# Layer 1 written out as four pipelines, layer 2's constants loaded inside it, and reciprocal square roots by Newton steps

## The chip, the cores and the metric

One Trainium2 chip; the program runs on 1 core. The core's engines each work through a queue of their own: TensorE (PE: matmuls and transposes; its weight loads are listed as PEld), VectorE (DVE), ScalarE (ACT), GpSimd (POOL) and SyncE (SP, which here only issues transfers). A result passes between engines through SBUF or through TensorE's accumulator banks (PSUM), and a semaphore tells the next engine that it is there. The metric is the device time of one execution in microseconds.

## The reference

The program is a network of four layers on x of shape (2, 64, 64, 128): two images, 64 x 64 positions, 128 channels. Cut to what the change touches:

```python
# layer 1: x = x + L1(groupnorm(x)), 32 groups of 4 channels
def L1(x):                                   # (b, 64, 64, 128)
    xn = layer_norm(x, norm_a, norm_b)       # over the 128 channels
    left  = (xn @ Wl + bl) * sigmoid(xn @ Wlg + blg)
    right = (xn @ Wr + br) * sigmoid(xn @ Wrg + brg)
    out_gate = sigmoid(xn @ Wog + bog)
    out = einsum('bkjd,bkid->bijd', left, right) / 64
    out = layer_norm(out, on_a, on_b) * out_gate
    return out @ Wo + bo

# layer 2, attention: t = t + L2(layer_norm(t)), t = x as (2, 4096, 128), 4 heads of 32
def L2(x):
    q, k, v = silu(x @ Wq + bq), silu(x @ Wk + bk), silu(x @ Wv + bv)
    u = x @ Wu + bu
    pos = einsum('nm,bmd->bnd', pos_w[4095 + m - n], v)      # Toeplitz, not causal
    s = where(causal, (q @ k.T / sqrt(32)) ** 2, 0)
    a = concat(silu(s) @ v, pos)
    a = layer_norm(a) * ln_gamma + ln_beta
    return relu(u * a @ Wf + bf) + x
```

Layer 0 is a groupnorm and a softmax attention with relative positions over the 4096 positions, layer 2 has an expert layer behind the attention, and layer 3 is an attention and an expert layer. Each of them starts with a norm, so each needs 1/sqrt(variance + eps). Everything is in float32.

## The kernel before

x stays in SBUF throughout, as 64 tiles of 128 positions x 128 channels. The layers run one after the other; the order of the work on each engine is mostly the order in which the program issues it, as a scheduler places it, and inside layers 0 and 2 it is written out by generators that yield between pieces (a stage's filling work is cut in pieces, and so many pieces are issued between two steps of the main loop).

**1/sqrt** is `rstd_parts`, lines 95 to 112. VectorE adds eps (line 101, tile rs_v), ScalarE takes the square root (line 105, rs_s), VectorE takes the reciprocal (line 108, rs_r) and sharpens it by one Newton step of three operations (lines 110 to 112). ScalarE holds one set of function tables at a time, and going from the sigmoid, silu or exponential to the square root and back shows as an ACT_TABLE_LOAD. `ln_stats` (lines 149 to 159) calls it for n tiles at once, after a pair of bn_stats and bn_aggr (lines 155, 156) for each; `group_scale` calls it for a groupnorm on 128x1.

**Layer 1** (lines 1044 to 1186) has five stages.
- Normalisation, lines 1067 to 1104. For each of the two images: `group_stats` transposes 32 tiles and takes their statistics, and two matmuls spread mean and scale over all partitions (line 1071, l1pb), which VectorE copies to gb (line 1079). Then four groups of 8 tiles: VectorE subtracts the mean (line 1083, l1y), POOL multiplies by the scale (line 1089), VectorE takes the row statistics and normalises (line 162), TensorE transposes (line 1098, l1pt), ScalarE writes xnT with norm_a and norm_b (line 1102).
- Projections, lines 1110 to 1126, 64 steps j. The weights of both matmuls are the columns j, j+64, ... of xnT, a strided read. VectorE adds the biases (lines 1117, 1118), ScalarE takes two sigmoids (1119, 1120), VectorE multiplies left and right by their gates into lr, with stride 64 (line 1121).
- Triangle product, lines 1129 to 1147: 256 matmuls of 64 x 64 x 64 for each of both halves, evicted by ScalarE (line 1142).
- Output norm, lines 1149 to 1169, 8 groups of 8: row statistics, 8 normalisations, multiplication by on_a and addition of on_b on VectorE (lines 1155, 1158), the gate product on POOL (line 1161), transposes (1166) and their copies on ScalarE (1167).
- Output projection, lines 1171 to 1186: 16 groups of 4 matmuls (l1o); POOL adds bo to x (line 1183), VectorE adds the result (line 1186).

**Layer 2's attention** starts with its constants (lines 1237 to 1278): a reversed position table of 2 MB is loaded (rev), TensorE flips it with an anti-diagonal matrix (line 1263, l2flip), and VectorE writes it less its last value to toe (line 1264). `l2_folded` (lines 1189 to 1228) loads six small tensors and folds ln_gamma, ln_beta, Wu and Wf into wuy and buy (l2fT, l2ub, l2fy). Then come the weights and biases of q, k and v. The main loop goes over 16 blocks of 512 queries; scores are evicted by VectorE (line 1551) or ScalarE (line 1541) into l2es, POOL squares some of them in place (line 1554), ScalarE applies silu (line 1565), and TensorE multiplies by v (line 1579). Each block ends with a norm that calls `rstd_parts` on 128x4.

Of the kernel before, what the change touches and what calls it, by code (L numbers as in the profile page):

```python
# [8 lines left out]
F32 = mybir.dt.float32  # L9
AF = mybir.ActivationFunctionType  # L10
ALU = mybir.AluOpType
# [3 lines left out]
P = 128  # L15
# [23 lines left out]
class Net:  # L39
# [57 lines left out]
    def rstd_parts(self, out, var, eps, n, apart=False):  # L97
# [6 lines left out]
        s = self.small.tile([P, n], F32, tag=f"rs_s{n}", name="rs_s", bufs=4 if n < 8 else 2)  # L104
        nc.scalar.activation(s, v, AF.Sqrt)
        yield
        r = self.small.tile([P, n], F32, tag=f"rs_r{n}", name="rs_r", bufs=4 if n < 8 else 2)
        nc.vector.reciprocal(r, s)
        q = self.small.tile([P, n], F32, tag=f"rs_q{n}", name="rs_q", bufs=4 if n < 8 else 2)
        nc.vector.scalar_tensor_tensor(q, r, -0.5, r, ALU.mult, ALU.mult)  # L110
        nc.vector.tensor_tensor(q, q, v, ALU.mult)
        nc.vector.scalar_tensor_tensor(out, q, 1.5, r, ALU.add, ALU.mult)
# [48 lines left out]
    def normalize(self, out, src, mv, r, i):  # L161
        self.nc.vector.tensor_scalar(
            out, src, mv[:, i, 0:1], r[:, i : i + 1], ALU.subtract, ALU.mult
        )
# [879 lines left out]
    def layer1(self):  # L1044
        nc, tc, ins = self.nc, self.tc, self.ins
        with ExitStack() as st:
            wp = st.enter_context(tc.tile_pool(name="l1w", bufs=1))
            ps = st.enter_context(tc.tile_pool(name="l1p", bufs=3, space=PSUM))
# [16 lines left out]
            xnT = big.tile([P, B * L], F32, tag="a", name="l1xnT")  # L1065
            with tc.tile_pool(name="l1y", bufs=2) as yp:
                for b in range(B):
                    gm, gr = self.group_stats(ps, b)
# [9 lines left out]
                    gb = yp.tile([P, 2, C], F32, tag="gb", name=f"l1gb{b}")  # L1078
                    nc.vector.tensor_copy(gb.rearrange("p i c -> p (i c)"), pb[:, : 2 * C])
                    for g in range(4):  # L1080
                        ch = b * NC + 8 * g
                        y = yp.tile([P, 8, C], F32, tag="y", name=f"l1y{b}_{g}")
                        nc.vector.tensor_tensor(
                            y,
                            self.x[:, ch : ch + 8, :],
                            gb[:, 0, :].unsqueeze(1).broadcast_to([P, 8, C]),
                            ALU.subtract,
                        )
                        nc.gpsimd.tensor_tensor(
                            y, y, gb[:, 1, :].unsqueeze(1).broadcast_to([P, 8, C]), ALU.mult  # L1090
                        )
                        mv, r = self.ln_stats(y, 8, 1e-5, f"l1_{b}_{g}")
                        for half in range(2):
                            pt = ps.tile([P, 512], F32, tag="misc", name=f"l1pt{b}_{g}_{half}")
                            for k in range(4):
                                i = 4 * half + k
                                self.normalize(y[:, i, :], y[:, i, :], mv, r, i)
                                nc.tensor.transpose(
                                    pt[:, k * P : (k + 1) * P], y[:, i, :], self.ident
                                )  # L1100
                            at = (ch + 4 * half) * P
                            nc.scalar.activation(
                                xnT[:, at : at + 512], pt, AF.Identity, bias=nb, scale=na
                            )


            lr = big.tile([P, 2, C, S], F32, tag="lr", name="lr")
            gate = big.tile([P, S, C], F32, tag="gate", name="gate")
            with tc.tile_pool(name="l1t", bufs=3) as tp:
                for j in range(S):  # L1110
                    rows = xnT[:, j::S]
                    p1 = ps.tile([P, 512], F32, tag="misc", name=f"l1p1_{j}")
                    nc.tensor.matmul(p1, lhsT=rows, rhs=wcat[:, :512], start=True, stop=True)
                    p2 = ps.tile([P, C], F32, tag="og", name=f"l1p2_{j}")
                    nc.tensor.matmul(p2, lhsT=rows, rhs=wcat[:, 512:], start=True, stop=True)
                    t = tp.tile([P, 5 * C], F32, tag="t", name=f"l1t{j}")
                    nc.vector.tensor_tensor(t[:, :512], p1, bcat[:, :512], ALU.add)  # L1117
                    nc.vector.tensor_tensor(t[:, 512:], p2, bcat[:, 512:], ALU.add)
                    nc.scalar.activation(t[:, 256:512], t[:, 256:512], AF.Sigmoid)
                    nc.scalar.activation(gate[:, j, :], t[:, 512:], AF.Sigmoid)  # L1120
                    nc.vector.tensor_tensor(
# [4 lines left out]
                    )  # L1126

            tri = big.tile([P, S, C], F32, tag="a", name="tri")
            for d8 in range(C // 8):
                pt = ps.tile([P, 8, S], F32, tag="misc", name=f"l1tri{d8}")  # L1130
                for k in range(8):
# [10 lines left out]
                nc.scalar.activation(  # L1142
                    tri[:, :, 8 * d8 : 8 * d8 + 8].rearrange("p j d -> p d j"),
                    pt,
                    AF.Copy,
                    scale=1.0 / S,
                )
            yT = big.tile([P, B * S, S], F32, tag="lr", name="l1yT")
            for g in range(S // 8):
                js = slice(8 * g, 8 * g + 8)  # L1150
                mv, r = self.ln_stats(tri[:, js, :], 8, 1e-5, f"l1o{g}")
                for i in range(8):
                    self.normalize(tri[:, 8 * g + i, :], tri[:, 8 * g + i, :], mv, r, i)
                tj = tri[:, js, :]
                nc.vector.tensor_tensor(
                    tj, tj, ona.unsqueeze(1).broadcast_to([P, 8, C]), ALU.mult
                )
                nc.vector.tensor_tensor(
                    tj, tj, onb.unsqueeze(1).broadcast_to([P, 8, C]), ALU.add
                )  # L1160
                nc.gpsimd.tensor_tensor(tj, tj, gate[:, js, :], ALU.mult)
# [1057 lines left out]
```

## Time and profile before

| | |
|---|---|
| time, median of 3 runs | 4488.38 us (4481.65 to 4494.05) |
| the profiled execution's own time | 4491.71 us |
| its span on the profile | 4489.8 us |
| mean granted TensorE clock | 0.938 |
| TensorE (PE) busy | 4093.3 us (91%) |
| VectorE (DVE) busy | 2932.6 us (65%) |
| ScalarE (ACT) busy | 2488.6 us (55%) |
| GpSimd (POOL) busy | 912.0 us (20%) |
| layer 0 | 0 to 1606.6 us |
| layer 1 | 1606.6 to 1903.6 us |
| layer 2's constants | 1903.6 to 1946.6 us |
| layer 2's attention, main loop | 1946.6 to 3106 us |
| the rest | 3106 to 4489.8 us |

In a line of the profile, L1117 is line 1117 of the kernel, and out<-in names the tile written and the tiles read, with partitions x elements. A group's line gives how many instructions there were, their busy time in us and the mean of one in ns, and then how long the engine was idle just before them and what ended that. A table by stage gives for each stretch its length and each engine's busy time, with the granted TensorE clock and the share of time in which the DMA engines were busy. A busy TensorE is not TensorE at its peak.

### The profile page before, as it was taken

Reading aid. Unit: us, or ns where it says so; the run is one execution under the profiler, and the core shown is the slowest. Engines: PE = TensorE matmul, PEld = TensorE weight load, DVE = VectorE, ACT = ScalarE, POOL = GpSimd, SP = SyncE. Lnnn points to the kernel's source line nnn. Section 1 sums busy time; section 2 is a strip of 40 time slices with the busy share of each in tenths; the row PEclk is TensorE's granted clock in tenths of the full one; section 3 lists DMA queues with packets and bytes.
Section 4 is the critical chain, followed back from the end, with each engine's and each line's share of the span. In section 5 each row is a group of like instructions: output and inputs, shape, how many; then the busy total and the mean of one; then the engine's idle time right before and its main releaser. Section 6 shows DMA issues by size and latency. Waiting matters only on the chain.

```text
span 4489.8 us, 66995 instructions
## 1 busy us (share of the span) xinstructions
PE 4093.3 (91%) x26440; PEld 1633.4 (36%) x26440; DVE 2932.6 (65%) x4641; ACT 2488.6 (55%) x3267; POOL 912.0 (20%) x667
## 2 busy tenths in 40 slices
PE   6999999999999948468999899998689999999979
PEld 3233333333333326322233223332364444444453
DVE  4888888998999979745566656656253333333358
ACT  3777777777777724235777688785123222322225
POOL 4110011020000030113455455552000000000015
PEclk7999999999999968678999999997889999999969
DMA  6453335454333300000000000002610000000001
GB/s 174 93 135 62 69 84 137 76 123 89 59 60 61 61 9 1 10 18 1 1 1 1 1 1 1 1 1 88 177 40 0 0 0 1 0 0 1 0 10 34
DMA packets 200764, 189.10 MB, mean 42 GB/s; under 512 B 83546, under 2 KB 137658, under 8 KB 200250
## 3 DMA queue, kind: packets, MB, share of 16 engines
q1 hardware_dynamic: 196986, 179.35, 18.1%
q10 hardware_dynamic: 3072, 4.34, 0.4%
q8 instruction: 210, 3.44, 0.3%
q0 software_dynamic: 384, 1.05, 0.1%
q14 instruction: 112, 0.92, 0.1%
HBM read 143.78 MB, written 45.09 MB: 42 GB/s over the span
## 4 chain that ended last, share of the span: by engine, by line
PE 47%; DVE 9%; ACT 4%; issue 1%; SPq 1%; DMA 1%; POOL 0%; DVEq 0%; ACTq 0%; POOLq 0%
PE oTl L1954 10%; PE scl L1937 10%; PE l2sc L1527 5%; PE l2pos L1428 5%; PE l2av L1579 5%; PE f3ex L2121 2%; ACT l2es L1565 2%; SPq L1682 1%; PE l2pu L1412 1%; DVE l2es L1551 1%; DVE l1t L1117 1%; ACT l2es L1541 1%; PE l2po L1486 1%; PE l3pq L1889 1%; PE prl L1976 1%
## 5 line engine op out<-in xcount | busy, mean ns | idle before, releaser
L813 DVE TENSOR_TENSOR l0acc<-l0acc,l0es 128x1024 f32<-128x1024 f32 x960 | 1230.6, 1282 | 133.1 <-ACT l0es L808 39.3
L808 ACT ACTIVATE l0es<-l0sc 128x1024 f32<-128x1024 f32 x1024 | 952.4, 1053 | 284.7 <-PE l0sc L800 267.8
L800 PE MATMUL l0sc<-l0mv,ka 64*64 64x512 f32 x8192 | 921.7, 596 | 21.1 <-DMA l0mv<-l0hd 16.3
L1962 DVE TENSOR_TENSOR accl<-accl,esl 128x1024 f32<-128x1024 f32 x240 | 294.0, 1225 | 520.1 <-ACT esl L1948 482.1
L1554 POOL TENSOR_TENSOR l2es<-l2es 128x1024 f32<-128x1024 f32 (+3 forms) x288 | 505.0, 1753 | 603.9 <-DVE l2es L1551 532.8
L1948 ACT ACTIVATE esl<-scl 128x1024 f32<-128x1024 f32 x240 | 245.5, 1023 | 547.0 <-PE scl L1937 547.0
L1565 ACT ACTIVATE l2es<-l2es 128x1024 f32<-128x1024 f32 (+3 forms) x576 | 533.3, 977 | 6.9 <-POOL l2es L1558 6.7
L800 PEld LDWEIGHTS l0sc<-l0mv,ka 64*64 64x64 f32 x8192 | 294.5, 132 | 640.9 <-ACT l0es L808 296.8
L1551 DVE TENSOR_SCALAR l2es<-l2sc 128x1024 f32<-128x1024 f32 (+3 forms) x272 | 306.4, 1126 | 297.2 <-PE l2sc L1527 294.5
L1937 PE MATMUL scl<-l3qT,l3kT 128*128 128x512 f32 x1024 | 482.4, 593 | 0.9 <-DVE l3v L1903 0.9
L831 PE MATMUL l0o<-l0es,l0v 128*32 128x512 f32 x4096 | 465.6, 595 | 0.0
L1954 PE MATMUL oTl<-esl,l3v 128*128 128x512 f32 x960 | 448.5, 592 | 0.0
L1541 ACT ACTIVATE l2es<-l2sc 128x1024 f32<-128x1024 f32 (+3 forms) x288 | 273.4, 949 | 261.3 <-PE l2sc L1527 258.2
L1527 PE MATMUL l2sc<-l2q,l2kT 32*128 32x512 f32 (+3 forms) x2304 | 340.5, 625 | 10.0 <-DVE l2es L1551 5.8
L1579 PE MATMUL l2av<-l2es,l2v 128*32 128x512 f32 (+3 forms) x2304 | 321.6, 579 | 8.8 <-ACT l2es L1565 8.7
L1428 PE MATMUL l2pos<-l2v,toe 128*32 128x512 f32 (+3 forms) x2304 | 299.5, 581 | 1.4 <-ACT l2v L1373 1.4
L745 POOL TENSOR_TENSOR l0os<-l0os,l0rr 128x512 f32<-128x512 f32 x32 | 63.2, 1975 | 1152.0 <-ACT l0rr L742 1091.3
L2133 POOL TENSOR_TENSOR f3part<-f3part 128x256 f32<-128x256 f32 x64 | 46.5, 726 | 1204.3 <-ACT f3part L2130 1204.3
L1937 PEld LDWEIGHTS scl<-l3qT,l3kT 128*128 128x128 f32 x1024 | 192.2, 190 | 231.1 <-issue 226.5
L1954 PEld LDWEIGHTS oTl<-esl,l3v 128*128 128x128 f32 x960 | 182.4, 190 | 229.6 <-issue 225.5
L831 PEld LDWEIGHTS l0o<-l0es,l0v 128*32 128x32 f32 x4096 | 121.4, 109 | 304.1 <-issue 299.5
L1527 PEld LDWEIGHTS l2sc<-l2q,l2kT 32*128 32x128 f32 x2304 | 100.9, 189 | 255.0 <-ACT l2es L1565 91.7
(468 smaller groups left out, 3915.6 us busy)
## 6 DMA issues: line engine op xcount, KB each, us to landing
l0mv<-l0hd SPq DMA_DIRECT2D x254, 128.0 KB
l0mv<-l0qd SPq DMA_DIRECT2D x124, 256.0 KB
f2w<-in_L_ffn_weight_dram SPq DMA_DIRECT2D x16, 1024.0 KB
f2w<-in_L_ffn_weight_dram SPq DMA_DIRECT2D x64, 256.0 KB
l0mv<-l0wd SPq DMA_DIRECT2D x126, 128.0 KB
l0sh<-l0eh SPq DMA_DIRECT2D x60, 144.0 KB
l0tw<-l0sw SPq DMA_DIRECT2D x64, 128.0 KB
l0wd<-l0rw SPq DMA_DIRECT2D x16, 512.0 KB
```

Of the source, the lines that this page charges most:

```text
L800: nc.tensor.matmul(sc[64 * c : 64 * c + 64, h, :], lhsT=ka[rows, k0 : k0 + 64], rhs=mv[rows, NX - 1 - yb, :], start=True, stop=True,)
L808: nc.scalar.activation(es[yb, s], sc, AF.Exp)
L813: nc.vector.tensor_tensor(cur.acc, cur.acc, es[yb, s], ALU.add)
L831: nc.tensor.matmul(cur.o[lo : lo + HD, :], lhsT=v[:, 2 * (xb * NX + yb) + s, HD * h : HD * (h + 1)], rhs=es[yb, s][:, h, :], start=(xb == ...
L1428: nc.tensor.matmul(pos[c : c + 32, j0:, :], lhsT=toe[:, d * P + c : d * P + c + 32], rhs=v[:, n0 + j0 - d : n0 + 4 - d, :], start=(d == n0 ...
L1527: nc.tensor.matmul(sc[:, h2, off:], lhsT=kT[hs, cols], rhs=q[hs, off:], start=True, stop=True,)
L1551: nc.vector.tensor_scalar(es[:, :, lo:], sc[:, :, lo:], root, None, ALU.mult)
L1554: nc.gpsimd.tensor_tensor(part, part, part, ALU.mult)
L1565: nc.scalar.activation(e[:, :, off:], e[:, :, off:], AF.Silu)
L1579: nc.tensor.matmul(avs[i][hs, off:], lhsT=vs[b][:, k, hs], rhs=es[h // 2][:, h % 2, off:], start=(k == 0), stop=last,)
L1937: nc.tensor.matmul(sc[:, i, :], lhsT=kT[:, k * P : (k + 1) * P], rhs=qs, start=True, stop=True,)
L1954: nc.tensor.matmul(oT, lhsT=v[:, k, :], rhs=es[:, i, :], start=(k == 0), stop=(k == NC - 1),)
```

## The change

`rstd_parts` takes no square root on ScalarE any more: a first guess comes from the bits of the variance, read as an integer (one VectorE operation), and three Newton steps of three VectorE operations follow. It yields after the first of them.

`layers12` replaces layer1 and layer2_attn. It opens the pool of layer 2's constants first, and hands layer 1 a generator, `l2_constants`, which layer 1 runs inside its normalisation: the loads at its start (after layer 1's own, on SP's queue), the flips in the last three rounds of its loop, `l2_folded` after that, with its loads on ScalarE's queue. The table of 2 MB lies in the buffer that later holds lr.

Layer 1 is written in the order of emission (manual_schedule):
- normalisation: all of `group_stats` in pieces; then a loop over rounds s, in which POOL subtracts and multiplies for group s (shift), ScalarE writes xnT for group s-3 (turned), 6 of 8 normalisations of group s-2 are ScalarE's and 2 VectorE's (rows), and the row statistics are those of group s-1. There is a y buffer for each of the 8 groups and PSUM has 5 buffers instead of 3. xnT is written as [partition, j, image, i], so that a step's weights are contiguous.
- projections: the gate's bias addition goes straight to gate, the product into lr is POOL's, and POOL adds bo to x every fourth step.
- triangle product: evicted by VectorE and ScalarE in turn.
- output norm: a loop over rounds, with the 8 normalisations on ScalarE and the multiplication by on_a on POOL; on_b stays on VectorE and the gate product on POOL.
- output projection: without the addition of bo.

```diff
@@ rstd_parts
-        s = self.small.tile([P, n], F32, tag=f"rs_s{n}", name="rs_s", bufs=4 if n < 8 else 2)
-        nc.scalar.activation(s, v, AF.Sqrt)
-        yield
         r = self.small.tile([P, n], F32, tag=f"rs_r{n}", name="rs_r", bufs=4 if n < 8 else 2)
-        nc.vector.reciprocal(r, s)
+        nc.vector.tensor_scalar(
+            r.bitcast(mybir.dt.int32),
+            v.bitcast(mybir.dt.int32),
+            -0.5,
+            float(0x5F3759DF),
+            ALU.mult,
+            ALU.add,
+        )
         q = self.small.tile([P, n], F32, tag=f"rs_q{n}", name="rs_q", bufs=4 if n < 8 else 2)
-        nc.vector.scalar_tensor_tensor(q, r, -0.5, r, ALU.mult, ALU.mult)
-        nc.vector.tensor_tensor(q, q, v, ALU.mult)
-        nc.vector.scalar_tensor_tensor(out, q, 1.5, r, ALU.add, ALU.mult)
+        for i in range(3):
+            nc.vector.scalar_tensor_tensor(q, r, -0.5, r, ALU.mult, ALU.mult)
+            nc.vector.tensor_tensor(q, q, v, ALU.mult)
+            nc.vector.scalar_tensor_tensor(out if i == 2 else r, q, 1.5, r, ALU.add, ALU.mult)
+            if i == 0:
+                yield
@@ new helpers
+    def shifts(self, mv, r, n):
+        m = self.small.tile([P, n], F32, tag=f"lm{n}", name="lm")
+        self.nc.vector.scalar_tensor_tensor(m, mv[:, :, 0], -1.0, r, ALU.mult, ALU.mult)
+        return m
+
+    def normalize_act(self, out, src, r, m, i):
+        self.nc.scalar.activation(
+            out, src, AF.Identity, bias=m[:, i : i + 1], scale=r[:, i : i + 1]
         )
@@ layer 1, normalisation
+                def shift(s):
+                    b, g = divmod(s, 4)
+                    ch = b * NC + 8 * g
+                    for i, op in enumerate((ALU.subtract, ALU.mult)):
                         nc.gpsimd.tensor_tensor(
+                            ys[:, s],
+                            ys[:, s] if i else self.x[:, ch : ch + 8, :],
+                            gbs[b][:, i, :].unsqueeze(1).broadcast_to([P, 8, C]),
+                            op,
+                        )
...
+                for s in range(B * 4 + 3):
+                    if s == 1:
+                        group_rows(1)
+                    if s < B * 4:
+                        shift(s)
+                    if 3 <= s:
+                        turned(s - 3)
+                    if 2 <= s < B * 4 + 2:
+                        rows(s - 2)
+                    if 1 <= s <= B * 4:
+                        row_stats(s - 1)
+                    if s >= B * 4:
+                        next(constants, None)
+                for _ in constants:
+                    pass
@@ layer 1, projections
-                    rows = xnT[:, j::S]
+                    rows = xnT[:, j].rearrange("p b i -> p (b i)")
...
-                    nc.vector.tensor_tensor(
+                    nc.gpsimd.tensor_tensor(
                         lr[:, :, :, j],
                         t[:, :256].rearrange("p (s d) -> p s d", s=2),
                         t[:, 256:512].rearrange("p (s d) -> p s d", s=2),
                         ALU.mult,
                     )
+                    if j % 4 == 3:
+                        xs = self.x[:, j - 3 : j + 1, :]
+                        nc.gpsimd.tensor_tensor(
+                            xs, xs, bo.unsqueeze(1).broadcast_to([P, 4, C]), ALU.add
+                        )
@@ layer 1, output norm
+            for s in range(G8 + 3):
+                js = [slice(8 * (s - k), 8 * (s - k) + 8) for k in range(4)]
+                if 2 <= s < G8 + 2:
+                    tj = tri[:, js[2], :]
+                    nc.vector.tensor_tensor(
+                        tj, tj, onb.unsqueeze(1).broadcast_to([P, 8, C]), ALU.add
+                    )
+                    nc.gpsimd.tensor_tensor(tj, tj, gate[:, js[2], :], ALU.mult)
+                if s < G8:
+                    mv, r = self.ln_stats(tri[:, js[0], :], 8, 1e-5, f"l1o{s}")
+                    scales[s] = r, self.shifts(mv, r, 8)
...
+                if 1 <= s <= G8:
+                    r, m = scales.pop(s - 1)
+                    for i in range(8):
+                        row = tri[:, 8 * (s - 1) + i, :]
+                        self.normalize_act(row, row, r, m, i)
+                    tj = tri[:, js[1], :]
+                    nc.gpsimd.tensor_tensor(
+                        tj, tj, ona.unsqueeze(1).broadcast_to([P, 8, C]), ALU.mult
+                    )
```

## The prediction

> **What bounds the kernel now.** I read the page's busy shares first, then a table of busy time by stage, because one share for the program hides the stages that the change touches. TensorE is busy for 91% of the span. The stages (times are from the span's start):
>
> ```profile
> core 0: us, PE busy (x) PEld busy (x) DVE busy (x) ACT busy (x) POOL busy (x), PEclk, DMA share, GB/s
> 1606.60:1707.10 100.50, 31.27 (x144) 23.50 (x144) 82.41 (x284) 15.79 (x27) 39.79 (x24) 0.57 0.04 10
> 1707.10:1794.40 87.30, 85.25 (x256) 66.06 (x256) 82.59 (x192) 44.28 (x129) 0.00 (x0) 0.97 0.00 1
> 1794.40:1812.20 17.80, 16.70 (x512) 16.56 (x512) 0.00 (x0) 15.25 (x17) 0.00 (x0) 0.90 0.01 4
> 1812.20:1886.40 74.20, 15.75 (x64) 12.55 (x64) 68.53 (x248) 12.31 (x25) 18.71 (x8) 0.52 0.00 0
> 1886.40:1903.60 17.20, 16.33 (x128) 16.14 (x128) 13.88 (x42) 0.41 (x3) 0.61 (x4) 0.89 0.00 1
> 1903.60:1946.60 43.00, 24.34 (x58) 11.68 (x58) 13.81 (x28) 3.29 (x4) 0.23 (x1) 0.72 0.21 69
> 1946.60:3106.00 1159.40, 1070.70 (x7803) 342.85 (x7803) 685.72 (x1174) 851.44 (x965) 568.35 (x368) 0.96 0.00 1
> ```
>
> These are layer 1's normalisation (A), projections (B), triangle product (C), output norm (D) and output projection (E), then layer 2's constants (F) and attention (G). A and D are VectorE's (82% and 92% busy), B is TensorE's with VectorE close behind, F is nobody's, G TensorE's.
>
> Next, what VectorE's time in A and D consists of. Groups of instructions in A, then two lines of D (first number busy us, then mean ns):
>
> ```profile
> L110 DVE SCALAR_TENSOR_TENSOR rs_q<-rs_r 128x8 f32<-128x8 f32 x8 | 8.1, 1012 | 0.2
> L111 DVE TENSOR_TENSOR rs_q<-rs_q,rs_v 128x8 f32<-128x8 f32 x8 | 7.3, 908 | 0.2
> L155 DVE BATCH_NORM_STATS2 st_l<-l1y 128x6 f32<-128x128 f32 x64 | 16.3, 265 | 7.3 <-POOL l1y L1089 7.3
> ```
> ```profile
> L1161 POOL TENSOR_TENSOR tri<-tri,gate 128x1024 f32<-128x1024 f32 x8 | 18.7, 2338 | 166.9 <-DVE r_l1o L112 124.3 <-DVE tri L1158 42.6
> L101 DVE TENSOR_SCALAR rs_v<-mv_l1o 128x8 f32<-128x8 f32 x8 | 12.3, 1538 | 0.0
> L110 DVE SCALAR_TENSOR_TENSOR rs_q<-rs_r 128x8 f32<-128x8 f32 x8 | 1.3, 158 | 0.0
> ```
>
> An operation on 128x8 elements takes 158 ns alone and about 1 us where POOL runs. So a small VectorE operation waits for the POOL operation in flight, and one gets through per POOL operation. The timeline of layer 0's start shows it on 128x1 operands beside POOL operations of 2.0 us (start, duration):
>
> ```profile
> 2.56 32.17 POOL L301 TENSOR_TENSOR ka<-l0rev 32x1024 f32<-32x1024 f32 x16
> 18.97 0.16 DVE L108 RECIPROCAL rs_r<-rs_s 128x1 f32<-128x1 f32 x1 [0.27 <-ACT rs_s L105]
> 19.81 1.85 DVE L111 TENSOR_TENSOR rs_q<-rs_q,rs_v 128x1 f32<-128x1 f32 x1
> 21.69 1.85 DVE L112 SCALAR_TENSOR_TENSOR gr<-rs_q,rs_r 128x1 f32<-128x1 f32 x1
> 23.57 9.38 DVE L447 TENSOR_SCALAR l0mv<-l0xT,gm,gr 128x1024 f32<-128x1024 f32 x4
> ```
>
> Reciprocals and batch statistics pass (0.16 and 0.27 us), and so do reads of PSUM (L101 there, 0.16). The Trainium skill ("SBUF — State Buffer", Who interferes with whom) speaks of an exclusive lock on a port pair, held for a whole instruction, against VectorE operations with two SBUF inputs or in a 2-port mode. That is a rule against this change, which gives POOL more two-input work and VectorE more small SBUF operations; the rows agree on who is held, and it gives no price, so the sum by it alone would be the same.
>
> F, in the chain of work that ended last:
>
> ```profile
> 1904.25 8.09 DMA wq<-in_L_attn_Wq_dram
> 1912.34 10.20 PE l2flip L1263 x16
> 1924.35 4.14 DMA lb<-in_L_attn_ln_beta_dram
> ```
>
> **The change part by part.** The sum is made against the profiled execution, 4491.7 us, which is 3.3 above the median of the three runs, 4488.4.
>
> *Reciprocal square root everywhere.* Before: 5 VectorE operations and a ScalarE square root, with table loads of 1.28 us. After: 11 VectorE operations and none on ScalarE. Alone, a small operation follows another after about 0.2 us, so 6 more cost 1.2 us on VectorE; beside POOL each costs a POOL operation.
>
> Layer 0's start: from rs_v at 18.54, the 10 others except those after POOL's end at 34.7 get through at one per 2.0 us. Eight fit, so gr lands near 35.2 instead of 23.5. The four normalisations then run without POOL, at some 0.6–1.2 us instead of 2.35. The first projection matmul goes from 26.0 to about 36, but its 16 are then no longer paced by L447 (9.07 us before, 6.8 by 0.427 each), so the query projection starts at 42.9 instead of 34.9. Everything to the first scores (87.3) follows it through l0xT, POOL copies and a chain of DMAs; TensorE is full afterwards. **+8** (0 if the operations pass POOL, +11 if the matmuls gain nothing).
>
> G: sixteen joins, each with one chain of 128x4 operations and two table loads on ScalarE (2.57 us), which vanish. ScalarE loses 16 x 2.8 = 44 us of work, but it is 73% busy and TensorE waits for it (l2av on l2es, 8.7 us in all) and for VectorE behind it some 10 more; at most 12 come back. Against it, POOL's squares (1.9 us each, 49% of the stage) hold the small operations:
>
> ```profile
> L1554 POOL TENSOR_TENSOR l2es<-l2es 128x1024 f32<-128x1024 f32 x240 | 455.0, 1896 | 562.3 <-DVE l2es L1551 512.0 <-DVE rs_v L101 42.7 <-DVE rs_r L108 7.6
> L110 DVE SCALAR_TENSOR_TENSOR rs_q<-rs_r 128x4 f32<-128x4 f32 x16 | 19.1, 1196 | 0.5
> L111 DVE TENSOR_TENSOR rs_q<-rs_q,rs_v 128x4 f32<-128x4 f32 x16 | 10.3, 642 | 0.5
> ```
>
> Queued behind a held chain is L1551, which evicts the scores; POOL's next square waits for it, and TensorE for the score bank. The first piece grows by a held operation (1.85) and 0.6 of others, the second by 0.4 to 1.3, some 3.3 us a join on an engine 59% busy; of it up to 1.0 us reaches TensorE: 16, less 12 given back. **+4**, taken because the stage's waits for VectorE are short (13 waits of at most 0.9 us for l2es). Ends: -12 (nothing reaches TensorE) and +28 (2.5 us a join, the half of what all nine held at half a square each would be, less the 12).
>
> Layer 2's expert layer: per group of 8 rows 6 more operations of 0.2 us; VectorE is busy 10.4 of each 12.7 us there, no POOL. Eight chains are 9.6 us, half of it hidden in VectorE's waits for the softmax (12.1 us in eight): **+5** (0 to 11). Layer 3's two norms: +1.3 each for the chain, -1.5 for table load and square root: 0.
>
> *A.* POOL takes the subtraction too: 16 operations of 2.34 us instead of 8, in a row. Start as before, 1621.5 (group statistics and the row broadcast are unchanged). First 8: until 1640.5; meanwhile VectorE's second group chain gets about 8 held operations through, one each, and is done near 1642.6. Second 8: until 1661.6, while the first row chain gets about 8 of its 12 through; it ends near 1662.5. Then seven groups without POOL: 8 pairs of statistics (2.1), 12 small operations (2.46), 2 normalisations (0.53), 5.2 us each, against 9.95 before: 1699. The other 6 normalisations are ScalarE's, 6 x 0.29 in 5.2. After the last: transposes and the strided evacuation 6.5, then six constant loads on ScalarE's queue, which stands behind that evacuation; before, from their first issue to the end of l2fy took about 9. The projections stand behind l2fy in TensorE's queue: they start near 1715 instead of 1707. **+8** (-22 if nothing were held: 1669 for the last group; +14 if copies and loads run at their slowest rows).
>
> *B.* Weights contiguous: loads of 184–190 ns instead of 313 and 296, which ran over. The period of 1.29 us falls to TensorE's 1.07 to 1.15. VectorE loses the strided product (0.64). POOL gets it, 64 x 128x256, and 16 additions of 1.26: with 0.73 (L2133, contiguous, same size) 1.05 us a step, just beside TensorE. 64 x 1.2 = 77–81: **-8** (-12; +7 if the strided write takes 1.1, as strided copies do in L577, 1047 ns at the least for 128x512). The Trainium skill ("GPSIMD Engine Reference", Performance versus the Vector engine) has elementwise work some twice as fast on VectorE and a floor of 2.5 cycles an element with two inputs. The rows agree that POOL is the slower engine; by the skill's floor B would be as here, not the +7.
>
> *C.* Evacuations on two engines, but TensorE has 16.7 of 17.8: **-0.5**.
>
> *D.* VectorE loses 8 normalisations and one 1.2 us operation per group, and POOL gets it. Per group of the pipeline: addition 1.2; the gate product (2.34) runs under the statistics and holds rs_v; the ona product (2.35) holds the next one; then ten free ones (2.05): 8.1 against 8.7 before, with filling and draining 72.6: **-2** (-18 unheld, +5 if one more operation is held per group).
>
> *E.* Same TensorE work: 0.
>
> *F.* Gone from here: constants, flips (10.2) and the folded loads lie under A, where TensorE has 69 us free and the DMA share is 0.04. On SP's queue the loads stand behind layer 1's own. Without that cover the 8.1 of the load, 10.2 of flips and 4.1 of lb would come back, 22. What is left after the last output matmul (1902.8): one addition 0.8, ten small operations 2.0, and from xn_0k to the first scores 14.8, that is 17.6 instead of 43.7: **-26** (-30 to -20).
>
> **Sum:** 8 + 4 + 5 + 8 - 8 - 0.5 - 2 - 26 = -11.5, so 4480. I give 4479, between that and the same step taken from the median.
>
> **The rivals.**
> 1. *VectorE is held less than one operation per POOL operation.* For it: L110 and L112 in A average 1.0 and 0.6 us, less than a product of 2.34. Against it: the 1.85 us rows. If half of the hold is real, A gives -7, D -10, layer 0's start +4: 4480 - 15 - 8 - 4 = 4453.
> 2. *Slower: the chains stall TensorE in layer 2.* One mechanism: nine more two-input operations on VectorE between two squares of POOL, with L1551 behind them. For it: the L110 and L111 rows, 43 us of POOL idling for rs_v. Against: VectorE has 474 us free there. Price: 2.5 us a join less 12 given back is +28 rather than +4: 4504. It decides from 2.4 us a join on.
> 3. *POOL bounds B.* The strided product at 1.1 us instead of 0.73 makes a step 1.41 us: +7 rather than -8, 4495. Decides from 0.8 us on.
>
> **How the numbers follow.** What a measurement here can tell from no change is 0.3%, 13.5 us: faster is below 4475, slower above 4502. My own case has 0.40, with 4468 to 4492 as its range (a quarter to a third of it below 4475); rival 1 has 0.27, all faster; rival 2 has 0.23, all but a little slower; rival 3 has 0.10, part of it slower. Faster 0.13 + 0.27 + 0.01 = 0.41; slower 0.22 + 0.04 = 0.26; the rest 0.33. The range leaves a tenth at each end: from 4446, below rival 1's middle, to 4512, above rival 2's.
>
> **What would show it.** Right: F's 43 us as 17 or 18; B's step near 1.2 us with weight loads of 190 ns; in A sixteen POOL operations in a row from 1621 with small VectorE operations of 1.5–2.3 us under them; gr of layer 0 near 35 and first scores near 95; D's period near 8. Wrong: small operations of 0.2 us beside a running POOL product (rival 1), TensorE's waits in G for l2es and l2av above 40 us (rival 2), the POOL product of B above 0.8 us (rival 3), or projections that wait for lb or toe until after 1720.

## The result, and the profile after

The changed kernel takes 4463.2 us (median of 10 runs, 4455.9 to 4479.4); the kernel before, 4488.2 (10 runs, 4481.7 to 4496.6). The ratio is 0.9949, with a 95% interval of 0.9937 to 0.9961: 25 us or 0.5% faster. The forecast was 4479, with 4446 to 4512 as its range. The profiled execution took 4462.9 us, with a span of 4459.7.

The table of busy time by stage, cut where the stages of the changed kernel begin and end (A, B, C, D, E, F, G as before):

```profile
core 0: us, PE busy (x) PEld busy (x) DVE busy (x) ACT busy (x) POOL busy (x), PEclk, DMA share, GB/s
1622.10:1732.70 110.60, 45.88 (x171) 29.77 (x172) 92.48 (x306) 36.82 (x66) 38.18 (x20) 0.58 0.12 36
1732.70:1804.70 72.00, 70.11 (x259) 38.92 (x258) 57.23 (x130) 40.47 (x129) 63.44 (x80) 0.99 0.00 1
1804.70:1822.40 17.70, 16.66 (x512) 16.52 (x512) 8.29 (x8) 8.40 (x8) 1.13 (x1) 0.90 0.01 3
1822.40:1896.90 74.50, 15.78 (x65) 12.58 (x65) 58.98 (x233) 34.85 (x80) 37.30 (x16) 0.53 0.00 1
1896.90:1914.30 17.40, 16.64 (x128) 16.45 (x128) 13.95 (x45) 0.00 (x0) 0.00 (x0) 0.87 0.00 1
1914.30:1930.60 16.30, 11.29 (x28) 5.78 (x28) 7.35 (x24) 3.29 (x4) 0.00 (x0) 0.79 0.00 0
1930.60:3087.70 1157.10, 1070.35 (x7805) 349.70 (x7804) 726.13 (x1290) 804.21 (x910) 568.50 (x368) 0.97 0.00 1
```

A is longer by 10 us, B shorter by 15, F shorter by 27. Layer 1 begins 15.5 us later than it did.

Half of that is layer 0's start. Lines of its timeline, with six of the chain's eleven operations beside POOL (start, duration):

```profile
18.55 0.16 DVE L101 TENSOR_SCALAR rs_v<-gpv 128x1 f32<-128x1 f32 x1 [0.74 <-PE gpv L453]
18.74 0.15 DVE L105 TENSOR_SCALAR rs_r<-rs_v 128x1 int32<-128x1 int32 x1
19.81 1.85 DVE L116 TENSOR_TENSOR rs_q<-rs_q,rs_v 128x1 f32<-128x1 f32 x1
21.70 1.85 DVE L117 SCALAR_TENSOR_TENSOR rs_r<-rs_q,rs_r 128x1 f32<-128x1 f32 x1
25.46 0.16 DVE L116 TENSOR_TENSOR rs_q<-rs_q,rs_v 128x1 f32<-128x1 f32 x1
31.23 1.85 DVE L117 SCALAR_TENSOR_TENSOR gr<-rs_q,rs_r 128x1 f32<-128x1 f32 x1
33.12 2.98 DVE L464 TENSOR_SCALAR l0mv<-l0xT,gm,gr 128x1024 f32<-128x1024 f32 x4
```

The scale is there at 33.1 instead of 23.5 us, the four normalisations then run unheld (0.7 us each), and the first scores come at 94.9 instead of 87.3.

In A, three lines of VectorE's first row chain and the POOL operations beside them:

```profile
1660.90 2.19 DVE L115 SCALAR_TENSOR_TENSOR rs_q<-rs_r 128x8 f32<-128x8 f32 x1
1663.12 2.26 DVE L116 TENSOR_TENSOR rs_q<-rs_q,rs_v 128x8 f32<-128x8 f32 x1
1665.42 0.17 DVE L117 SCALAR_TENSOR_TENSOR rs_r<-rs_q,rs_r 128x8 f32<-128x8 f32 x1
```
```profile
1660.70 2.36 POOL L1129 TENSOR_TENSOR l1y<-l1y,l1gb 128x1024 f32<-128x1024 f32 x1
1663.03 2.33 POOL L1129 TENSOR_TENSOR l1y<-x,l1gb 128x1024 f32<-128x1024 f32 x1
1665.44 2.35 POOL L1129 TENSOR_TENSOR l1y<-l1y,l1gb 128x1024 f32<-128x1024 f32 x1
```

Each held operation ends just as a POOL operation does; in the gap of 0.08 us a second one slips in at 0.17. This chain takes 16.7 us for its twelve operations (seven of them held); each later one, without POOL, 2.4.

In B, the groups of instructions (first number busy us, then mean ns) show why it shrank: weight loads of 191 and 193 ns instead of 296 and 313, and a POOL product of 739 ns:

```profile
L1198 PEld LDWEIGHTS l1p<-wcat,l1xnT 128*128 128x128 f32 x128 | 24.5, 191 | 31.0 <-issue 30.8 <-DVE gate L1201 0.2
L1196 PEld LDWEIGHTS l1p<-wcat,l1xnT 128*128 128x128 f32 x127 | 19.5, 193 | 0.0
L1204 POOL TENSOR_TENSOR lr<-l1t 128x256 f32<-128x256 f32 x64 | 45.6, 739 | 64.0 <-ACT l1t L1202 63.9
```

Around F, the chain of work runs from the last output matmul straight into layer 2, with no load and no flip in it:

```profile
1909.97 3.59 PE l1o L1277 x32
1913.56 2.96 issue
1916.52 1.07 PE l2t_0k L1452 x4
1918.36 2.06 PE l2pk L1465 x2
```

### The profile page after: what moved, and what is told of

It reads as the page before. It is cut to its first block, busy times and chain, and to the rows that moved or that the text cites. A ratio compares the mean times of both kernels' runs of the same rounds, so it can differ in the third digit from the quotient of the medians.

```text
span 4459.7 us, 67181 instructions
## 1 busy us (share of the span) xinstructions
PE 4074.5 (91%) x26440; PEld 1608.8 (36%) x26440; DVE 2959.4 (66%) x4783; ACT 2461.1 (55%) x3275; POOL 987.5 (22%) x747
## 3 DMA queue, kind: packets, MB, share of 16 engines
q0 software_dynamic: 384, 1.05, 0.1%
## 4 chain that ended last, share of the span: by engine, by line
PE 47%; DVE 8%; SPq 1%; ACT 1%; issue 1%; DMA 0%; POOL 0%; DVEq 0%; ACTq 0%; POOLq 0%
PE oTl L2062 10%; PE scl L2045 10%; PE l2sc L1635 6%; PE l2pos L1536 5%; PE l2av L1687 5%; PE f3ex L2229 2%; DVE l2es L1659 2%; SPq L1790 1%; PE l2pu L1520 1%; PE l2po L1594 1%; PE l3pq L1997 1%; PE f3pl L2163 1%; PE prl L2084 1%; DVE l2a L1573 0%; DVE st_l2o L1570 0%
## 5 line engine op out<-in xcount | busy, mean ns | idle before, releaser
L1635 PE MATMUL l2sc<-l2q,l2kT 32*128 32x512 f32 (+3 forms) x2304 | 356.7, 618 | 14.6 <-DVE l2es L1659 6.3
L1687 PE MATMUL l2av<-l2es,l2v 128*32 128x512 f32 (+3 forms) x2304 | 307.5, 575 | 0.8 <-ACT l2es L1673 0.7
```

The lines of the kernel that those rows point to most:

```text
L1635: nc.tensor.matmul(sc[:, h2, off:], lhsT=kT[hs, cols], rhs=q[hs, off:], start=True, stop=True,)
L1687: nc.tensor.matmul(avs[i][hs, off:], lhsT=vs[b][:, k, hs], rhs=es[h // 2][:, h % 2, off:], start=(k == 0), stop=last,)
```

## The experiments

Times are medians, to be held against 4463.2 for the changed kernel; stage times are from each run's own trace. One execution's trace scatters by several us in places that the change does not touch; the two repeats show how far.

### Square root back in layer 0

```diff
-                yield from self.rstd_parts(gr, pv[:, 0, 0:1], 1e-5, 1, apart=True)
+                yield from self.rstd_parts(gr, pv[:, 0, 0:1], 1e-5, 1, apart=True, sqrt=True)
```

> The changed kernel, with the old square root on ScalarE and one Newton step put back in layer 0's groupnorm alone; all other norms keep three Newton steps. The traces have the first scores of layer 0 at 94.9 us after against 87.3 before (+7.6), and layer 0 ends another 7.8 later. Theory A (the held Newton chain delays the start, and the late start is also what costs the second 7.8): first scores back at 87, layer 0 back at 1606 for its end, the kernel 15 us below the changed one, about 4448. Theory B (only the start is the chain's; the second 7.8 is something else, or chance of one execution): first scores at 87, the kernel 7 to 8 below, about 4455. Rival (the start is not bound by this chain): no change, 4463.

Measured 4456.3 us (0.9936 of before, 0.9919 to 0.9953), 7 below the changed kernel. The first scores are back at 87.2, but from there to the last ones it takes 1505.8 us, against 1508.8 in the changed kernel's trace and 1500.9 in the first trace of before. Theory B: the chain costs the start and nothing behind it.

### Constants behind layer 1

```diff
-            scratch = big.tile([P, 2 * C * S], F32, tag="lr", name="l2scratch")
-            constants = between(ps, scratch)
-            next(constants)
...
                 nc.vector.tensor_tensor(xs, xs, pt, ALU.add)
+            scratch = big.tile([P, 2 * C * S], F32, tag="lr", name="l2scratch")
+            for _ in between(ps, scratch):
+                pass
```

> The changed kernel, with layer 2's constants loaded, flipped and folded behind layer 1's output projection instead of inside its normalisation. My theory: the stretch from the last addition of layer 1 to the first scores of layer 2 goes from 17 back to about 43 us (+26); the projections of layer 1 start some 9 sooner, because nothing stands between the last evacuation and them (the 6.3 us of loads and folding, 2.8 us of evictions); net +17, about 4480. Rival (the constants were hidden anyway by layer 1's end, and the gain there has another cause): stretch stays near 17, kernel 9 below the changed one, about 4454.

Measured 4478.3 us (0.9982, 0.9969 to 0.9994), 15 above. From the first output matmul to the first scores it takes 53.2 us instead of 33.7, and A 102.5 instead of 110.6. So moving the constants gives 20 us at the one end and costs 8 at the other. The sign is as I expected; the stretch is not back at its old length (60.0): the kernel before has 6 us of issue and loading of ln_beta behind the flips in its chain of work, and this run has none.

### Strided weights again

```diff
-                    rows = xnT[:, j].rearrange("p b i -> p (b i)")
+                    rows = xnT[:, j::S]
```

with xnT written as before the change.

> The changed kernel, with xnT in its old layout, so that the projections' weights are a strided read again; the product into lr stays on POOL. My theory (the weight loads set the step): weight loads back to about 300 ns and the step from 1.08 back to 1.29 us, 64 x 0.21 = +13, less some 1 us for the faster evacuation: about 4475. Rival (VectorE, with the strided product of 0.64 us, set the step before, and moving it is what gave the 15 us of this stage): the step stays at 1.08 to 1.13, within 3 us of the changed kernel, about 4464.

Measured 4479.9 us (0.9985, 0.9974 to 0.9995), 17 above; B takes 86.2 us against 72.0. The groups of B in this run:

```profile
L1194 PEld LDWEIGHTS l1p<-wcat,l1xnT 128*128 128x128 f32 x128 | 37.8, 295 | 18.3 <-issue 1.9
L1192 PEld LDWEIGHTS l1p<-wcat,l1xnT 128*128 128x128 f32 x128 | 34.1, 314 | 0.0
L1196 DVE TENSOR_TENSOR l1t<-l1p,bcat 128x512 f32<-128x512 f32 x64 | 44.3, 692 | 27.5 <-PE l1p L1192 26.7 <-PE l1p L1194 0.8
```

VectorE is idle 27.5 us for TensorE, and the old step is back without the old product on VectorE. The weight loads alone are enough to bring it back. Whether the gain of B also needed the product off VectorE is not shown by any run.

### Square root back in layer 2's attention

```diff
-                yield from self.rstd_parts(rs[i], mv[:, :, 1], 1e-3, 4)
+                yield from self.rstd_parts(rs[i], mv[:, :, 1], 1e-3, 4, sqrt=True)
```

and the same for its first norm.

> The changed kernel, with the old square root in layer 2's attention alone (its first norm and the sixteen joins), so with the table loads there. My reading of the two traces (the main loop went from 1138.6 to 1135.1 us: waits of TensorE for ScalarE's silu fell from 8.7 to 0.8, waits for the held chain rose by some 4): loop +3.5 us, about 4467, with 32 table loads and waits for silu back near 9. Rival 1 of the prediction's kind (held chains cost more than the table loads): the loop gets shorter by 5 or more, about 4458 or below.

Measured 4453.4 us (0.9925, 0.9908 to 0.9941), 10 below. The loop takes 1150.8 us, with TensorE's waits for silu back at 8.5 us, and is still 4.5 shorter than the changed kernel's 1155.3. My reading of the two traces fell: the loop of the changed kernel was not shorter because of the Newton steps, but in spite of them. Rival 1's sign is right and its size nearly. Another 4 us come with the first norm's longer chain (29.7 us from the first output matmul to the first scores, not 33.7).

### Square root back everywhere

```diff
-        mv, r = self.ln_stats(tri[:, js[0], :], 8, 1e-5, f"l1o{s}")
+        mv, r = self.ln_stats(tri[:, js[0], :], 8, 1e-5, f"l1o{s}", True)
```

and so at every other call.

> The changed kernel with the old square root put back in every norm; pipelines, layout and constants stay as changed. My theory (three Newton steps cost time wherever VectorE sets the pace or POOL runs beside it): layer 0's start -7.6; layer 1's normalisation -15 (fewer held operations in the second group's chain and the first row chain, about 0.75 us less in each of seven groups); output norm -6 (a period of 7.4 instead of 8.1); layer 2's attention -4.5; its expert layer -2.7: together -36, about 4428. Rival (only layer 0 and layer 2 pay, the rest is hidden): -12, about 4451. Second rival (the table loads that come back eat it): no faster than 4463.

Measured 4459.8 us (0.9939, 0.9922 to 0.9955). A is 97.5 us instead of 110.6 and the expert layer's statistics 41.3 instead of 46.0, as expected; but triangle product and output norm take 110.2 instead of 92.2. Groups of the output norm in this run:

```profile
L106 ACT ACTIVATE rs_s<-rs_v 128x8 f32<-128x8 f32 x8 | 1.7, 209 | 50.6 <-DVE rs_v L101 50.6
L1272 POOL TENSOR_TENSOR tri<-tri,ona 128x1024 f32<-128x1024 f32 x8 | 18.7, 2341 | 58.2 <-ACT tri L190 58.2
L1253 DVE TENSOR_TENSOR tri<-tri,onb 128x1024 f32<-128x1024 f32 x8 | 9.8, 1226 | 41.1 <-POOL tri L1272 41.1
```

They read as a circle. ScalarE waits 50.6 us at the square root for VectorE's statistics, with the eight normalisations of the group before, which are ready, queued behind it; POOL waits 58.2 for those; VectorE's addition waits 41.1 for POOL; and the statistics stand behind that addition. The period is 11.4 us instead of 8.1. The table loads are not the cause: only one of 1.3 us falls in this stage. In this order of emission the Newton steps are what lets the pipeline run; an order with the normalisations ahead of the square root was not tried.

### Newton steps alone, on the kernel before

```diff
-        nc.scalar.activation(s, v, AF.Sqrt)
...
+        for i in range(3):
```

> The kernel before, with the three Newton steps alone. My theory: layer 0's start +8, layer 2's attention +4.5, its expert layer +2.7, layer 1's normalisation +10 to +25 (six more operations in each of eight chains, beside POOL), output norm +8 (8.7 to 9.7 a group): +33 to +48, about 4520 to 4535. Rival (the table loads saved pay for the steps): 4488 or below.

Measured 4515.5 us (1.0064, 1.0047 to 1.0081), 30 above the kernel before, just under the low end: start +8, A +11, triangle product and output norm +5, G +4, expert statistics +3 against the two traces of before. The table loads saved do not pay for the steps.

### The product into lr back on VectorE

```diff
-                    nc.gpsimd.tensor_tensor(
+                    nc.vector.tensor_tensor(
                         lr[:, :, :, j],
```

> The changed kernel with the product into lr back on VectorE; weights stay contiguous, the addition of bo stays on POOL. The run with strided weights gave a step of 1.32 us, so the weight loads alone account for the old step. If VectorE also needed 1.29 us a step (0.69 + 0.28 + 0.64 less some overlap of issue), the step is 1.3 here as well: +13, about 4476 (theory A: two limits side by side, and both parts of the change were needed). Theory B (VectorE had room): step 1.08 to 1.12, 4463 to 4466.

Measured 4522.2 us (1.0085, 1.0068 to 1.0102), 59 above; both theories missed. B takes 109.6 us, at 1.66 us a step, because the order of emission puts the product of step j ahead of step j+1's additions in VectorE's queue, and it waits there for ScalarE's sigmoid (the wait is 23.7 us in sum, and TensorE's second matmul waits 17.8 for the gate's addition behind it). So the run does not say what VectorE's product cost in the old order. It shows another thing in A, which is 12 us longer though no line of it is changed. POOL's queue there:

```profile
1672.14 2.35 POOL L1129 TENSOR_TENSOR l1y<-l1y,l1gb 128x1024 f32<-128x1024 f32 x1
1674.45 19.58 POOL L1212 TENSOR_TENSOR x<-x,bo 128x512 f32<-128x512 f32 x16
```

With no product to wait for, POOL does all sixteen additions of bo right behind A's operations, for 20 us. VectorE's next chain is held by them, one operation to an addition, and takes 13.8 us instead of 2.4:

```profile
1680.67 1.18 DVE L105 TENSOR_SCALAR rs_r<-rs_v 128x8 int32<-128x8 int32 x1
1683.11 1.19 DVE L116 TENSOR_TENSOR rs_q<-rs_q,rs_v 128x8 f32<-128x8 f32 x1
```

### The kernel before, and the changed one, once more

> The kernel before once more, unchanged, for a second trace of it. The first trace has the 128 small matmuls of layer 2's expert layer at a granted clock of 0.60 (25.0 us) where every trace with the change has 1.00 (15.3 us), and TensorE 7 us busier in layer 2's main loop than one with the same waits. Theory A (the clock is a matter of the execution): the second trace differs from the first in these places, by up to 10 us each. Theory B (it belongs to the old kernel): 25 us and 1069 us busy again.

> The changed kernel once more, unchanged, for a second trace. In layer 2's main loop ten traces show two patterns of granted clock, 7 us apart at equal waits (0.69 to 0.79 in the second 20 us, or 0.86 to 0.88). Theory A (the pattern is a matter of the execution): it may fall either way here, and stages differ by up to 10 us from the first trace only where the clock or layer 0's transfers do. Theory B (it belongs to the code): 1155.3 us again. The stages of layer 1 come out within 1 us of the first trace under both.

They took 4489.7 and 4462.9 us. The second trace of before has the expert layer's small matmuls at full clock, 15.3 us instead of 25.0. The stretch in the first trace of before, in its second, and in the first of the changed kernel, a line each:

```profile
3270.00:3300.00 30.00, 27.62 (x161) 26.28 (x159) 15.41 (x49) 0.27 (x1) 0.00 (x0) 0.60 0.01 3
```
```profile
3279.00:3300.00 21.00, 18.14 (x162) 16.43 (x160) 16.00 (x55) 0.70 (x3) 0.00 (x0) 1.00 0.02 5
```
```profile
3252.00:3273.00 21.00, 18.31 (x162) 16.58 (x162) 15.40 (x50) 0.27 (x1) 0.00 (x0) 1.00 0.03 8
```

Layer 0's main part took 1509.6 us in the second trace of before, 8.7 longer than in the first. The loop of layer 2 took the changed kernel 1155.3 us the first time and 1161.8 the second, with TensorE 6.5 us busier on as many matmuls:

```profile
1930.60:3085.90 1155.30, 1068.55 (x7799) 348.53 (x7798) 724.33 (x1280) 804.21 (x910) 568.50 (x368) 0.97 0.00 1
```
```profile
1924.20:3086.00 1161.80, 1075.02 (x7798) 349.34 (x7797) 724.52 (x1280) 804.62 (x910) 568.39 (x368) 0.96 0.00 1
```

All three are a matter of the execution, then (theory A in both): the 8 us in layer 0 behind its start, 10 us of clock in the expert layer, 7 in layer 2. Over fourteen traces the loop takes 1157.7 to 1158.1 or 1150.2 to 1150.8 us with the square root, and 1161.8 or 1155.2 to 1155.3 with the Newton steps (one 1152.6): at either clock pattern the steps cost 4 to 5 us. Layer 1's stages came within 1.5 us of the first trace, where 1 had been expected; B within 0.7.

### The subtraction back on VectorE

```diff
-                        nc.gpsimd.tensor_tensor(
+                        (nc.gpsimd if i else nc.vector).tensor_tensor(
```

> The changed kernel with the subtraction of layer 1's normalisation back on VectorE (128x1024, 1.2 us each), the multiplication on POOL. Theory A (POOL's sixteen operations in a row hold VectorE's chains, and that is what the stage loses): POOL runs 8 operations with gaps, the second group's chain (15.7 us from its statistics to gr in the changed kernel) and the first row chain (16.7 us) both shrink to about 8; VectorE gains 9.6 us of work: net -5, about 4458, stage 105. Theory B (VectorE's count of operations sets the stage, not the hold): +10, stage 120, about 4473.

Measured 4455.6 us (0.9930, 0.9913 to 0.9946). The second group's chain takes 5.5 us from its statistics to gr instead of 15.7, and the first row chain 2.4 instead of 16.7, with the Newton operations at 0.16 or 0.17 us. But the later groups, at 9.3 us against 6.1, give most of that back: VectorE has the subtraction to do itself (1.22 us), and its two normalisations are held by POOL's product (2.64 us for the two, against 0.59 in the changed kernel):

```profile
1657.14 2.39 POOL L1129 TENSOR_TENSOR l1y<-l1y,l1gb 128x1024 f32<-128x1024 f32 x1 [6.90 <-DVE l1y L1129]
1666.43 2.39 POOL L1129 TENSOR_TENSOR l1y<-l1y,l1gb 128x1024 f32<-128x1024 f32 x1 [6.90 <-DVE l1y L1129]
```
```profile
1655.84 1.22 DVE L1129 TENSOR_TENSOR l1y<-x,l1gb 128x1024 f32<-128x1024 f32 x1
1656.98 2.64 DVE L169 TENSOR_SCALAR l1y<-l1y,mv_l,r_l 128x128 f32<-128x128 f32 x2
```

A is 107.5 us, 2 to 3 less than in the two traces of the changed kernel. Theory A named the hold rightly and oversold what it was worth; the rest of the 8 us lies in stages that scatter.

### Newton steps only where they pay

```diff
-                    gm, gr = self.group_scale(ps, b, sts[b])
+                    gm, gr = self.group_scale(ps, b, sts[b], True)
-                    mv, r = self.ln_stats(ys[:, s], 8, 1e-5, f"l1_{s}")
+                    mv, r = self.ln_stats(ys[:, s], 8, 1e-5, f"l1_{s}", True)
```

and so in layer 0, layer 2's attention and its expert layer; the output norm and layer 3 keep the steps.

> The changed kernel with the Newton steps kept only in layer 1's output norm (and layer 3's two norms), the old square root everywhere else. In the run with the square root everywhere, layer 1's normalisation took 97.5 us instead of 110.6, layer 2's expert statistics 41 instead of 46, but the output norm with the triangle product 110 instead of 92, because the square root stands behind eight normalisations in ScalarE's queue. Theory A (the price of the Newton steps depends on the stage: a loss wherever ScalarE has room, a gain in the output norm): -7.6, -13, -4.5, -4.7 against the changed kernel, none in the output norm: about 4433. Theory B (the 18 us of the output norm have another cause, such as what the faster stages ahead leave to it): output norm again near 110, about 4455.

Measured 4429.2 us: 0.9869 of before (0.9853 to 0.9886), 34 us below the changed kernel. Its stages A to G:

```profile
1609.80:1708.40 98.60, 45.48 (x171) 29.61 (x172) 78.49 (x246) 40.17 (x78) 38.14 (x20) 0.60 0.14 40
1708.40:1781.30 72.90, 71.01 (x259) 39.40 (x258) 57.37 (x130) 39.41 (x128) 63.53 (x80) 0.98 0.00 1
1781.30:1799.00 17.70, 15.12 (x512) 14.98 (x512) 9.63 (x15) 8.42 (x8) 1.14 (x1) 1.00 0.01 3
1799.00:1871.90 72.90, 15.74 (x64) 12.54 (x64) 57.64 (x226) 34.88 (x81) 37.27 (x16) 0.51 0.00 0
1871.90:1889.00 17.10, 16.26 (x128) 16.07 (x128) 13.67 (x42) 1.66 (x3) 0.00 (x0) 0.89 0.00 1
1889.00:1901.80 12.80, 9.48 (x32) 4.70 (x32) 5.98 (x15) 3.18 (x4) 0.00 (x0) 0.87 0.00 0
1901.80:3052.00 1150.20, 1062.05 (x7798) 341.58 (x7798) 684.11 (x1164) 851.15 (x964) 568.49 (x368) 0.97 0.00 1
```

Triangle product and output norm are at 90.6 us. Theory A: the price of the steps belongs to the stage. (In ScalarE's queue the square root stands ahead of the eight normalisations, as the run with square roots everywhere shows, not behind them.) Against the kernel before, the layout, the constants and the pipelines, with the steps in the output norm, are worth 59 us; the steps everywhere else take 34 of them back.

A further run goes on from this one:

```diff
-                nc.scalar.dma_start(out=t, in_=src)
+                nc.sync.dma_start(out=t, in_=src)
...
                     if s == 1:
                         group_rows(1)
+                        for _ in constants:
+                            pass
```

> As e9, and the rest of layer 2's constants moved: the six folded loads go on SP's queue behind the others, flips and folding are issued right after the second group's chain, where VectorE is held by POOL anyway. With nothing between the last evacuation and the projections, they start 8 us sooner (the run without the constants there had them start 102.5 us after the stage's start instead of 110.6): about 8 below e9, 4425. If VectorE is delayed by the evictions instead (8 x 0.75), only 2 of the 8 are left: 4431.

Measured 4433.1 us (0.9877, 0.9861 to 0.9894): A is 95.2 us instead of 98.6, and the time is not to be told from the run before it. The 3.4 us gained in A are nearer the lesser of the two cases, and 4429 is the best of this study.

## Why the prediction was right, and where it was off

Direction and range held; the size did not: 9 us faster was forecast, less than half of the 25 that came. The time lies outside the 4468 to 4492 that I gave to my own case. The stated range held it because its low end stood for rival 1, whose mechanism was not at work; that is luck. Taking both traces of each kernel together, so that what scatters with the execution weighs less (in G, where both traces of before have the slower clock pattern, the second pair sets the changed kernel against the runs with the square root):

| step | forecast | measured | from |
|---|---|---|---|
| layer 0's start | +8 | +7.9 | first scores 87.3, 87.6 to 94.9, 95.8 |
| A | +8 | +9.1 | 100.4, 101.7 to 110.6, 109.6 |
| B | -8 | -15.8 | 87.3, 87.6 to 72.0, 71.3 |
| C and D | -2.5 | -0.6 | 92.1, 92.0 to 92.2, 90.7 |
| E and F | -26 | -27.0 | 60.0, 60.6 to 33.7, 32.9 |
| G, at equal clock pattern | +4 | +4 to +5 | 1158 to 1162; 1150.5 to 1155.3 |
| expert statistics | +5 | +3.3 | 43.3, 42.2 to 46.0, 46.1 |
| sum | -11.5 | -19 | |

The sum of -19 lies within what the runs allow (0.9937 to 0.9961 is -28 to -17). What remains up to 25 can be the chances of the clock and of layer 0; that was not separated further.

- *B is the step that failed, a term mis-sized.* I gave 1.2 us a step, from a TensorE bound of 1.07 to 1.15 and a POOL of 1.05 beside it, and multiplied it out to 77 to 81. The step measured 1.08, TensorE's bound itself: 64 of them and 3 us. POOL's 4.2 us per four steps fit beside it without friction, and the strided write cost it nothing (739 ns, 726 for the contiguous row of that size). My margin for two engines side by side had no row behind it.
- *Layer 0's start* came out to 0.1 us, but by two errors that cancel. gr was ready at 33.1 and not 35.2, as two operations of the ten passed at 0.15 to 0.16 us; and the sixteen key projections behind it took 8.8 us (34.0 to 42.8), not the 6.8 that I gave them. Putting the square root back there returned the first scores to 87.2.
- *A* went as worked out up to the end of the first row chain. POOL started at 1637.4, which is 1621.9 when the later start of 15.5 us is taken off (forecast 1621.5); it ended at 1677.2, or 1661.7 (1661.6). Behind it two errors cancel in part. Each of the seven later groups took 6.1 us and not 5.2, since eight pairs of statistics and their aggregation take 3.2 in this order and not 2.1: the last chain ended at 1704.8 by that clock (1699). The transposes, evacuations, loads and folding after it took 12 us and not 16, so the projections began at 1717.2 (1715). One term was wrong without mattering: ScalarE's normalisation takes 0.48 us and not 0.29.
- *D*: the period is 8.1 us as forecast. It fills more slowly than I allowed; TensorE waits 18.2 us for the first group.
- *F*: 16.3 us, or 17.4 from the last output matmul, for 17.6. Behind it stands a price in A of 8, which the run with late constants shows and which my +8 for A held.
- *G*: I forecast +4 as 16 less 12. The net came out; its terms did not, and that they cancel is luck. TensorE's waits for silu fell by 8 us (8.7 to 0.8), not 12, so the chains cost some 12. About half of these show as waits, 3.7 of them of score matmuls for the chain. The rest is in TensorE's busy time: between the run with the steps in the output norm alone and the changed kernel its idle time in the loop falls by 1.4 us (1150.2 less 1062.1, to 1155.3 less 1068.6), and its busy time grows by 6.5 on as many matmuls. What lengthens it is not shown. On VectorE the chain grew by 41 us, 2.6 a join where I had 3.3, and nearly half of that is one operation that I had not singled out, the integer guess in the place of the reciprocal (the changed kernel's line, then that of before):

```profile
L105 DVE TENSOR_SCALAR rs_r<-rs_v 128x4 int32<-128x4 int32 x16 | 21.6, 1349 | 0.5
```
```profile
L108 DVE RECIPROCAL rs_r<-rs_s 128x4 f32<-128x4 f32 x16 | 2.7, 167 | 0.0
```

- *Rival 1* (0.27) is refuted: held operations ran 1.85 to 2.3 us, one to each POOL operation in A. *Rival 2* (0.23) decided from 2.4 us a join on and is refuted; the steps do cost TensorE time there, some 0.8 us a join, 0.3 net of what came back. *Rival 3* (0.10) is refuted by the 739 ns. The time of 4463 lies between my own case and rival 1, but by B's gain, not by a weaker hold.

The rule of the Trainium skill that spoke against the change ("SBUF — State Buffer", Who interferes with whom) held for scalar_tensor_tensor and tensor_tensor where POOL ran beside them: up to 1.85 us in layer 0's start, 2.27 in A and 1.89 in G, against 0.16 or 0.17 without POOL.

## What to carry to other kernels

A chain of small operations must be priced by what runs on the neighbour that can hold it: the same twelve operations cost 2.4 us alone and 16.7 beside POOL. Replacing a square root on another engine by a longer chain on the busy one paid here only where the square root's place in that engine's queue stopped a pipeline, which is a question for each stage and not for the helper that all stages share. And before reading a gain from two traces, look at a second trace of the same kernel: here, 10 us of clock in the expert layer and 9 us in layer 0 would have been booked to the change.

## What had not been expected of the hardware

- The integer step of the guess (tensor_scalar on int32) was held or not by its width. On 128x1 it took 0.15 us with a POOL operation running, in layer 0's start and in A, where the next line took 0.85 and 1.18. On 128x4 it took 1.88 or 1.89 us in eleven of layer 2's sixteen joins; on 128x8, 2.30 us once in the output norm, and 1.18 beside POOL's additions in the run with the product back on VectorE. The reciprocal that it replaces passed a running POOL operation at 0.17 us on 128x4 and 0.20 on 128x8, so the exchange added a held operation.
- In A, POOL's subtraction and the product behind it lie 0.08 us apart. In that gap the held operation ends and a second one goes through, so that only two of three operations pay.
- TensorE ran matmuls back to back for 22 us at half clock in the first trace of before, and the same 128 matmuls at full clock in thirteen other traces. What decides it was not found.

```profile
3277.00:3299.00 22.00, 22.00 (x107) 21.89 (x106) 12.45 (x39) 0.00 (x0) 0.00 (x0) 0.50 0.01 1
```
